# A block's scatters as a list of steps of their own at the end of each slot

## The chip, the cores and the metric

The kernel runs on one core of a Trainium2 chip. The metric is the device time of one execution in microseconds, where lower is better. A core has a matrix engine (TensorE, PE in the profile, with its weight loads as PEld), a vector engine (VectorE, DVE), a scalar engine (ScalarE, ACT) and a general engine (GpSimd, POOL). Each works through its own queue of instructions in order. SyncE (SP) issues most of the transfers; POOL issues the indirect ones, in which every row has an address of its own.

## The reference

The reference is one Macaron layer on 4096 tokens with 256 features:

```python
x = x + 0.5 * ffn(layernorm(x))
x = x + attention(layernorm(x))
x = x + 0.5 * ffn(layernorm(x))
```

The attention works in groups of 64 tokens with 16 heads of 16 features, a causal mask, and an RMS norm over q and over k with a learned weight. The same FFN is used twice. It is a mixture of experts:

```python
shared = silu(x @ sg) * (x @ su) @ sd                   # hidden width 2048
probs  = softmax(rmsnorm(x) @ router_w.T)               # 8 experts
topk_p, topk_i = top_k(probs, 2)
rw     = topk_p / sum(topk_p)
dispatch[e] = first 640 of the tokens that chose e      # capacity 640
eout   = silu(xg @ rg[e]) * (xg @ ru[e]) @ rd[e]        # xg = x[dispatch], width 1024
routed = scatter_add(eout * rw) ; ffn = shared + routed
```

## The kernel before

Every large product is made of three float16 products. An operand is split into a high part (`hi`, a cast on ACT) and a low part (`lo`, the difference between the value and its high part, on DVE or POOL), and the pairs hi·hi, hi·lo and lo·hi are summed in PSUM.

The 4096 tokens are 8 blocks of 512, and a block is 4 tiles of 128. There are four phases. In phase a the shared expert of the first FFN runs over blocks 0 to 3, while all 32 tiles go through the layer norm, the split, the transposition and the router. Phase b runs the first FFN's eight experts. Phase c runs the shared expert over blocks 4 to 7 of the first FFN and 0 to 6 of the second, while the 32 tiles go through the attention, the second layer norm and the second router. Phase d runs the second FFN's experts and its last shared block.

A shared block (`shared`) is a loop over 16 chunks of 128 hidden features. For each chunk `gate_up` makes two PSUM tiles `pgu` (L336). In phase a ACT takes the SiLU of the first (L347); in phase c it takes a tanh (L343) and DVE combines it (L344). DVE multiplies by the second (L349), ACT casts the high part `hh` (L351), DVE makes the low part `hl` (L352). The down product (`down`, L360) is put off behind the next chunk's gate and up. It adds into two PSUM accumulators `po`, which DVE reads at the end of a block (`xr`, L393).

Beside the shared expert run the tiles. Each tile is a list of steps (`tile1` in phase a, `attn_tile` with `tile2` in phase c), written as a generator. A slot (`Tiles.steps`) advances every list that is under way by one step. A new list begins every second slot in phase a (`GAP_A`) and every fourth in phase c (`GAP_C`). `drive` interleaves the main loop with the steps of a slot, two at a time, so the order in which the program is written mixes the two. The build then lets a scheduler set each engine's order from a model of the engines' times; `tc.issue_after(anchor)` keeps an instruction behind another one.

On POOL a tile of phase c has the layer norm's power (`stats`, L149, one for `mv`/`rstd` of the second FFN's norm, one for `amv`/`arstd` of the attention's), the low part of the normalized tile (`two`, L169, tiles `X`, `xa`, `yp`), the power of the q and k norm (L534, tile `ss`), three splits of q and k (L555 twice, L561 once, tile `QK`), the subtraction of the row maximum (L583, tile `S`) and the low part of the exponentials (L594, tile `e16`, `e` in the profile). DVE uses `rstd` in `nm` (L157) and `ss` in L544.

When a block's fourth tile has its router logits, `route` computes the two experts, their weights and the destination row of each token. Its last four steps are the scatters, one for each tile of the block: four copies on POOL put the token's number, its two weights and its expert into the tag columns of the tile `X` (L315), and two indirect transfers on POOL write the tile's rows to the experts' buffer `xg` in HBM (L317). An `X` tile is one of a ring of 16 in phase a and of 6 in phase c, and can be written anew when its two transfers have landed. A scatter stands behind the anchor, which is the last POOL split that the program has written; in phase a there is no such split.

Of the kernel before, what the change touches and what calls it, by code (L numbers as in the profile page):

```python
# [15 lines left out]
ALU = mybir.AluOpType  # L16
# [11 lines left out]
NB = 8  # L28
# [9 lines left out]
class Net:  # L38
# [102 lines left out]
    def stats(self, x, mv, rstd):  # L141
        nc = self.nc
        st = self.sm.tile([P, 6], F32, name="st")
        nc.vector.bn_stats(out=st, in_=x)  # L144
        nc.vector.bn_aggr(out=mv, in_=st)
        ve = self.sm.tile([P, 1], F32, name="ve")
        nc.vector.tensor_scalar(
            out=ve, in0=mv[:, 1:2], scalar1=LN_EPS, scalar2=1.0 / UP ** 2, op0=ALU.add, op1=ALU.mult)
        nc.gpsimd.tensor_tensor(out=rstd, in0=ve, in1=self.mhalf[:, :1], op=ALU.pow)  # L149

    def normed(self, x, mv, rstd, pool=False):

# [69 lines left out]
            fb["L"] = self.sm.tile([P, 4, E], F32, name="L")  # L222
        nc.scalar.copy(fb["L"][:, t, :], p)

    def route(self, R, b, fb):

        nc = self.nc
        sm = self.sm
        mv, rstd = fb["mv"], fb["rstd"]
        rs = sm.tile([P, 4], F32, name="rs")  # L230
        nc.gpsimd.tensor_tensor(out=rs, in0=rstd, in1=rstd, op=ALU.mult)
        nc.gpsimd.tensor_tensor(out=rs, in0=rs, in1=mv[:, :, 1], op=ALU.mult)
        nc.gpsimd.tensor_scalar_add(rs, rs, RMS_EPS * UP ** 2)
        nc.gpsimd.tensor_tensor(out=rs, in0=rs, in1=self.mhalf[:, :4], op=ALU.pow)
        L = fb["L"]
        mx = sm.tile([P, 4, E], F32, name="mx")
        ix = sm.tile([P, 4, E], U32, name="ix")
        for t in range(4):
            nc.vector.max(out=mx[:, t, :], in_=L[:, t, :])
            nc.vector.max_index(out=ix[:, t, :], in_max=mx[:, t, :], in_values=L[:, t, :])  # L240
        dl = sm.tile([P, 4], F32, name="dl")
        nc.vector.tensor_tensor(out=dl, in0=mx[:, :, 1], in1=mx[:, :, 0], op=ALU.subtract)
        nc.gpsimd.tensor_tensor(out=dl, in0=dl, in1=rs, op=ALU.mult)
        nc.gpsimd.tensor_scalar_mul(dl, dl, 1.0 / WS)
        nc.gpsimd.tensor_tensor(out=dl, in0=self.e1, in1=dl, op=ALU.pow)
        w1 = sm.tile([P, 4], F32, name="w1")
        nc.gpsimd.tensor_scalar_add(w1, dl, 1.0)
        nc.gpsimd.tensor_tensor(out=w1, in0=w1, in1=self.mone, op=ALU.pow)
        nc.gpsimd.tensor_scalar_mul(w1, w1, 0.5 / WS)
        nc.gpsimd.tensor_tensor(out=dl, in0=dl, in1=w1, op=ALU.mult)  # L250
        nc.gpsimd.tensor_tensor(out=w1, in0=w1, in1=dl, op=ALU.subtract)
        ef = sm.tile([P, 4, 2], F32, name="ef")
        nc.vector.tensor_copy(ef, ix[:, :, 0:2])
        yield
        oh = sm.tile([P, 4, 2, E], F32, name="oh")
        nc.vector.tensor_tensor(
            out=oh, in0=ef.unsqueeze(3).to_broadcast([P, 4, 2, E]),
            in1=self.iota8.unsqueeze(1).unsqueeze(1).to_broadcast([P, 4, 2, E]), op=ALU.is_equal)
        M = sm.tile([P, 4, E], BF16, name="M")
        nc.vector.tensor_tensor(out=M, in0=oh[:, :, 0, :], in1=oh[:, :, 1, :], op=ALU.add)  # L260
        yield
        pp = self.m1([P, 4, E], F32, "pp")
        nc.tensor.matmul(pp, lhsT=self.tri, rhs=M, start=True, stop=False)
        for t in range(1, 4):
            nc.tensor.matmul(pp[:, t:4], lhsT=self.ones, rhs=M[:, 0:4 - t], start=False, stop=False)
        nc.tensor.matmul(
            pp, lhsT=self.ones, rhs=R["run"].unsqueeze(1).to_broadcast([P, 4, E]), start=False, stop=True)
        n4 = sm.tile([P, E], F32, name="n4")
        nc.vector.tensor_reduce(out=n4, in_=M.rearrange("p t e -> p e t"), axis=AX.X, op=ALU.add)
        nc.vector.tensor_tensor(out=R["run"], in0=R["run"], in1=n4, op=ALU.add)  # L270
        pk = sm.tile([P, 4, 2, E], F32, name="pk")
        nc.vector.tensor_tensor(
            out=pk, in0=oh, in1=pp.unsqueeze(2).to_broadcast([P, 4, 2, E]), op=ALU.mult)
        pos = sm.tile([P, 4, 2], F32, name="pos")
        nc.vector.tensor_reduce(out=pos, in_=pk, axis=AX.X, op=ALU.add)
        yield
        df = sm.tile([P, 4, 2], F32, name="df")
        nc.vector.scalar_tensor_tensor(
            out=df, in0=ef, scalar=float(CAP), in1=pos, op0=ALU.mult, op1=ALU.add)
        nc.vector.tensor_scalar(  # L280
            out=pos, in0=pos, scalar1=float(CAP), scalar2=8192.0, op0=ALU.is_ge, op1=ALU.mult)
        nc.vector.tensor_tensor(out=df, in0=df, in1=pos, op=ALU.add)
        di = sm.tile([P, 4, 2], I32, name="di")
        nc.vector.tensor_copy(di, df)
        yield
        if b == NB - 1:
            self.limits(R)
            yield
        for t in range(4):
            with self.tc.issue_after(self.anchor.ins) if self.anchor else nullcontext():  # L290
                self.scatter(R, b, fb, t, di, w1, dl, ef)
            yield

# [212 lines left out]
    def attn_tile(self, R, j, x2, new_fb):  # L506

        nc = self.nc
# [6 lines left out]
        rstd = self.sm.tile([P, 1], F32, name="arstd")  # L515
# [12 lines left out]
        ss = self.sm.tile([P, 2], F32, name="ss")  # L528
        qk = a.tile([P, 2, H], F32, name="qk", tag="q32")
        for i in range(2):  # L530
            nc.scalar.activation(qk[:, i, :], pqk[:, i, :], AF.Square, scale=1.0 / XP, accum_out=ss[:, i:i + 1])
        nc.vector.tensor_scalar(
            out=ss, in0=ss, scalar1=XP ** 2 / H, scalar2=1e-6 * XP ** 2, op0=ALU.mult, op1=ALU.add)
        nc.gpsimd.tensor_tensor(out=ss, in0=ss, in1=self.mhalf[:, :2], op=ALU.pow)  # L534
        pv = self.m1([P, H], F32, "pv")
        self.project(pv, part, self.wqkv[:, :, :, 2 * H:], TERMS)
        vs = a.tile([P, 2, H], F16, name="vs")
# [2 lines left out]
            out=vs[:, 1, :], in0=pv, scalar=1.0 / XP, in1=vs[:, 0, :], op0=ALU.mult, op1=ALU.subtract)  # L540
        yield
        yield
        for i in range(2):
            nc.vector.scalar_tensor_tensor(  # L544
                out=qk[:, i, :], in0=pqk[:, i, :], scalar=ss[:, i:i + 1], in1=self.lnw,
                op0=ALU.mult, op1=ALU.mult)
        QS = self.QK[:, 0:16].rearrange("p (j s) (r a c) -> p j s r a c", s=2, r=2, a=4)
        for i in range(2):
            if i == 0:
                for r in range(2):  # L550
# [5 lines left out]
                        out=s[:, :, 2:4, :], in0=src, in1=s[:, :, 0:2, :], op=ALU.subtract)  # L556
            else:
# [4 lines left out]
                    out=s[:, :, 1::2, :], in0=src, in1=s[:, :, 0::2, :], op=ALU.subtract)  # L562
        yield
        QT = a.tile([P, 2, 24, 64], F16, name="QT")
        for g in range(2):
            nc.sync.dma_start_transpose(
                out=QT[:, g], in_=self.QK[g * 64:(g + 1) * 64].rearrange("p j c -> p (j c)"))
# [3 lines left out]
        for g in range(2):  # L571
            p = self.m1([P, 8, 64], F32, "psc")
            for jj in range(8):
# [4 lines left out]
                out=S[:, g * 8:(g + 1) * 8, :], in0=p,  # L578
                in1=self.mask.unsqueeze(1).to_broadcast([P, 8, 64]), op=ALU.add)
# [4 lines left out]
            out=S, in0=S, in1=mx.unsqueeze(2).to_broadcast([P, 16, 64]), op=ALU.subtract)  # L584
# [16 lines left out]
        for g in range(2):  # L601
# [7 lines left out]
            for r in range(2):  # L609
                sl = slice(r * 64, (r + 1) * 64)  # L610
                nc.vector.tensor_tensor(
                    out=Y[sl, g], in0=py[sl, :, r * 16:(r + 1) * 16],
                    in1=rc[sl].unsqueeze(2).to_broadcast([64, 8, 16]), op=ALU.mult)
# [58 lines left out]
class Tiles:  # L672
# [7 lines left out]
        self.nxt = 0  # L680

    def done(self):
        return self.nxt == self.count and not self.live

    def steps(self):

        if self.slot == self.nxt * self.gap and self.nxt < self.count:
            self.live.append(self.make(self.nxt))
            self.nxt += 1
        for g in list(self.extra):  # L690
            r = next(g, "end")
            if r == "end":
                self.extra.remove(g)
            elif r != "stall":
                yield
        for g in list(self.live):
            r = next(g, "end")
            if r == "end":
                self.live.remove(g)
            elif r == "stall":  # L700
                return
            yield
        self.slot += 1

# [35 lines left out]
def macaron(ctx, tc, x, w_qkv, ln_w, w_proj, router_w, rg, ru, rd, sg, su, sd, out):  # L740
    nc = tc.nc
    x = x.rearrange("b s h -> (b s) h")
    out = out.rearrange("b s h -> (b s) h")
    n = Net(ctx, tc)
# [4 lines left out]
    fbs = {}  # L749
# [11 lines left out]

    def tail(R, h, b, t):
        if t == 3:
            yield from n.route(R, b, fbs[(h, b)])

    def tile1(j):
        b, t = divmod(j, 4)
        y = n.load_tile(x, b, t)
        yield
        yield  # L770
        if b >= NA:
            nc.sync.dma_start(out=R1["acc"][j * P:(j + 1) * P], in_=y)
        yield from n.front_steps(y, t, new_fb(1, b))
        yield from tail(R1, 1, b, t)
        if j == 31:
            yield from n.expert_load(R1, 0, first[0])

    def tile2(j):
        b, t = divmod(j, 4)
        yield from n.attn_tile(R1, j, x2 if b < NC else out, new_fb(2, b))  # L780
        yield from tail(R2, 2, b, t)
        if j == 31:
            yield from n.expert_load(R2, 0, first[1])
# [8 lines left out]
    with n.phase("a", BT, 2, 16):  # L792
# [5 lines left out]
        tiles = Tiles(tile1, 32, GAP_A)  # L798
# [9 lines left out]
    with n.phase("c", BT, 2, 6, SLC):  # L808
        n.attn_init(w_qkv, ln_w, w_proj)
        tiles = Tiles(tile2, 32, GAP_C)  # L810
# [51 lines left out]
```

## Time and profile before

| | before |
|---|---|
| median of 3 runs | 1830.85 us (1830.73 to 1833.56) |
| the profiled execution | 1834.82 us |
| its span in the trace | 1833.1 us |
| mean granted clock of PE | 0.998 |
| PE busy | 1779.5 us |
| DVE busy | 1199.9 us |
| ACT busy | 952.9 us |
| POOL busy | 751.3 us |

The profile is of one execution. Its span leaves out 1.7 us of that execution's time, and busy times are sums over the span. The scatters' transfers take this much of POOL:

```profile
L317 POOL DMA_INDIRECT xg<-X,di x128 | 132.3, 1034 | 70.4 <-issue 27.5
```

In such a row stand the line, the engine and the operation, what is written from what, the number of instructions, then busy us, the mean ns of one, and last the engine's idle time just before them with what ended most of it. There are 128 of them: two transfers for each of 32 tiles in each of the two FFNs.

### The profile page before, as it was taken

The page shows a single profiled execution, that of the slowest core. Times are in us where ns is not written, and L with a number is a line of the kernel's source. Part 1 is how long each engine was busy: PE and PEld are TensorE (multiplying, and loading weights), DVE is VectorE, ACT ScalarE, POOL GpSimd, SP SyncE. Part 2 cuts the span into 40 slices and gives each one's busy share as a digit, 9 for nine tenths or more (in the row PEclk, how much of TensorE's full clock was granted, in tenths as well). Part 3 has the DMA queues.
Part 4 walks back from the last instruction along what each step waited for, and adds up shares of the span by engine and source line. Part 5 has one row for each costly group of instructions (what it writes and reads, how often), then busy time and mean ns, then how long its engine had stood idle before and what let it go on. Part 6 is the DMA issues. An engine that isn't in the chain of part 4 may idle for free.

```text
span 1833.1 us, 37526 instructions
## 1 busy us (share of the span) xinstructions
PE 1779.5 (97%) x13724; PEld 1197.0 (65%) x13724; DVE 1199.9 (65%) x2891; ACT 952.9 (52%) x2055; POOL 751.3 (41%) x1072
## 2 busy tenths in 40 slices
PE   7899999999999899999999999999999999999998
PEld 4555556777777556666666666665655677777765
DVE  7754445666666567878777878787656566666643
ACT  5433234555555366666666666666323455555542
POOL 6755530112211334567767676776430011112210
PEclk9999999999999999999999999999999999999999
DMA  7532042455543346668576776766213044455420
GB/s 219 146 90 77 3 88 54 107 118 124 118 113 90 73 77 112 122 118 146 113 146 124 133 142 117 144 101 126 52 27 80 28 111 111 107 120 122 102 47 12
DMA packets 439194, 185.96 MB, mean 101 GB/s; under 512 B 302305, under 2 KB 436125, under 8 KB 439008
## 3 DMA queue, kind: packets, MB, share of 16 engines
q1 hardware_dynamic: 420528, 161.60, 40.7%
q0 software_dynamic: 17664, 21.17, 6.5%
q8 instruction: 107, 1.75, 0.4%
q10 hardware_dynamic: 816, 0.79, 0.1%
q14 instruction: 79, 0.65, 0.1%
HBM read 78.95 MB, written 42.21 MB: 66 GB/s over the span
## 4 chain that ended last, share of the span: by engine, by line
PE 36%; issue 32%; POOL 12%; DVE 10%; DMA 5%; ACT 4%; SPq 0%; POOLq 0%; another core or an unknown queue 0%; DVEq 0%; ACTq 0%
PE pgu L336 22%; PE po L360 11%; POOL xg L317 3%; DVE sl L349 2%; DMA acc<-eo,eidscatter 2%; DVE sl L344 1%; DVE hl L352 1%; POOL X L315 1%; POOL rstd L149 1%; POOL acc L459 1%; ACT hh L351 1%; PE pqk L636 1%; POOL S L583 1%; DVE st L144 1%; POOL e L594 1%
## 5 line engine op out<-in xcount | busy, mean ns | idle before, releaser
L336 PE MATMUL pgu<-xb,sgu 128*128 128x512 f16 x3072 | 742.4, 380 | 18.1 <-DVE sl L349 7.7
L351 ACT CAST hh<-sl 128x512 f16<-128x512 f32 (+2 forms) x512 | 272.8, 533 | 482.9 <-DVE sl L349 466.6
L336 PE MATMUL pgu<-xe,wc 128*128 128x384 f16 (+1 forms) x3072 | 497.0, 299 | 0.0
L336 PEld LDWEIGHTS <-sgu 128*128 128x128 f16 x3072 | 293.4, 98 | 292.9 <-issue 25.8
L349 DVE SCALAR_TENSOR_TENSOR sl<-pgu,sl 128x512 f32<-128x512 f32 (+2 forms) x512 | 300.2, 587 | 227.3 <-PE pgu L336 193.4
L352 DVE TENSOR_TENSOR hl<-sl,hh 128x512 f16<-128x512 f32 (+2 forms) x512 | 311.2, 608 | 161.5 <-ACT hh L351 155.1
L360 PEld LDWEIGHTS <-hh 128*128 128x128 f16 x3328 | 320.3, 98 | 112.3 <-ACT hh L351 7.9
L336 PEld LDWEIGHTS <-wc 128*128 128x128 f16 x3072 | 300.5, 98 | 92.0
L360 PE MATMUL po<-sdw,hh 128*128 128x256 f16 x2048 | 350.1, 273 | 8.1 <-issue 2.8
L360 PE MATMUL po<-sdw,hl 128*128 128x256 f16 x1024 | 247.1, 273 | 14.3 <-DVE hl L352 13.4
L360 PE MATMUL po<-wd,hh 128*128 128x256 f16 x1280 | 223.6, 273 | 0.0
L459 POOL DMA_INDIRECT out_dram<-eo,eidscatter x40 | 65.1, 1627 | 342.1 <-DVE eo L458 332.3
L360 PEld LDWEIGHTS <-hl 128*128 128x128 f16 x1664 | 162.8, 98 | 58.6 <-DVE hl L352 24.2
L347 ACT ACTIVATE sl<-pgu 128x384 f32<-128x384 f32 (+1 forms) x336 | 158.9, 473 | 71.1 <-PE pgu L336 35.5
L459 POOL DMA_INDIRECT acc<-eo,eidscatter x40 | 65.7, 1643 | 296.5 <-DVE eo L458 286.8
L317 POOL DMA_INDIRECT xg<-X,di x128 | 132.3, 1034 | 70.4 <-issue 27.5
L360 PE MATMUL po<-wd,hl 128*128 128x256 f16 x640 | 152.5, 273 | 1.1 <-DVE hl L352 1.1
L344 DVE SCALAR_TENSOR_TENSOR sl<-sl,pgu 128x512 f32<-128x512 f32 x176 | 119.9, 681 | 48.1 <-ACT sl L343 46.1
L343 ACT ACTIVATE sl<-pgu 128x512 f32<-128x512 f32 x176 | 104.2, 593 | 45.3 <-PE pgu L336 39.7
L104 ACT ACTIVATE wc<-re 128x512 f16<-128x512 f32 x128 | 80.5, 629 | 67.9 <-PE pgu L336 57.6
L105 DVE SCALAR_TENSOR_TENSOR wc<-re,wc 128x512 f16<-128x512 f32 x128 | 88.3, 690 | 22.9 <-ACT wc L104 22.6
L583 POOL TENSOR_TENSOR S<-S,amx 128x1024 f32<-128x1024 f32 x32 | 62.0, 1938 | 79.0 <-DVE amx L582 72.1
(150 smaller groups left out, 1713.3 us busy)
## 6 DMA issues: line engine op xcount, KB each, us to landing
re<-in_L_ffn_rg_dram SPq DMA_DIRECT2D x128, 128.0 KB
re<-in_L_ffn_ru_dram SPq DMA_DIRECT2D x128, 128.0 KB
re<-in_L_ffn_rd_dram SPq DMA_DIRECT2D x128, 128.0 KB
y<-acc SPq DMA_DIRECT2D x64, 128.0 KB
y<-in_L_attn_x_dram SPq DMA_DIRECT2D x32, 128.0 KB
acc<-xr SPq DMA_DIRECT2D x16, 256.0 KB
out_dram<-xr SPq DMA_DIRECT2D x16, 256.0 KB
x<-y SPq DMA_DIRECT2D x28, 128.0 KB
```

The lines of the kernel that those rows point to most:

```text
L104: nc.scalar.mul(hi, src, WS)
L105: nc.vector.scalar_tensor_tensor(out=lo, in0=src, scalar=WS, in1=hi, op0=ALU.mult, op1=ALU.subtract)
L317: i = nc.gpsimd.indirect_dma_start(out=R["xg"][:, :], out_offset=bass.IndirectOffsetOnAxis(ap=di[:, t, k:k + 1], axis=0), in_=X, in_offset ...
L336: nc.tensor.matmul(p, lhsT=wc[:, w, i, k, :], rhs=x[:, 2 * a + k, :], start=(j == 0), stop=(j == 5))
L343: nc.scalar.activation(s, p, AF.Tanh, scale=0.5 / XP)
L344: nc.vector.scalar_tensor_tensor(out=s, in0=s, scalar=1.0, in1=p, op0=ALU.add, op1=ALU.mult)
L347: self.latest[0] = nc.scalar.activation(s, p, AF.Silu, scale=1.0 / XP).ins
L349: self.latest[1] = nc.vector.scalar_tensor_tensor(out=s, in0=ps[1], scalar=1.0 / XP / (2.0 * XP if tanh else 1.0), in1=s, op0=ALU.mult, op ...
L351: nc.scalar.copy(h[0], s)
L352: nc.vector.tensor_tensor(out=h[1], in0=s, in1=h[0], op=ALU.subtract)
L360: nc.tensor.matmul(o, lhsT=h[a][:, t * P:(t + 1) * P], rhs=wd[:, w], start=(c == 0 and j == 0 and t % 2 == 0), stop=(c == nch - 1 and j == 2),
L459: i = nc.gpsimd.indirect_dma_start(out=R["acc"][:, :], out_offset=bass.IndirectOffsetOnAxis(ap=ids[:, t:t + 1], axis=0), in_=eo, in_offset ...
```

## The change

The four scatters of a block become a list of steps of their own (`scatters`). For the blocks 0 to 6 `route` hands this list to the tiles' `extra` lists; for block 7 it still runs them as its own last steps. In a slot the lists under way are now advanced first, and each extra list is advanced by one step at the end of the slot, so one scatter is written per slot. Before, extra lists (none were used) came first. The tiles are done only when the extra lists are, too. The anchor is now also set by the powers of L149 and of L534, so a scatter stands behind the last power or split of its slot on POOL, and every scatter has an anchor, in phase a too.

```diff
@@ stats
-        nc.gpsimd.tensor_tensor(out=rstd, in0=ve, in1=self.mhalf[:, :1], op=ALU.pow)
+        self.anchor = nc.gpsimd.tensor_tensor(out=rstd, in0=ve, in1=self.mhalf[:, :1], op=ALU.pow)
@@ route
-    def route(self, R, b, fb):
+    def route(self, R, b, fb, tiles):
...
+        last = self.scatters(R, b, fb, di, w1, dl, ef)
+        if b == NB - 1:
+            yield from last
+        else:
+            tiles.extra.append(last)
+
+    def scatters(self, R, b, fb, di, w1, dl, ef):
+
         for t in range(4):
-            with self.tc.issue_after(self.anchor.ins) if self.anchor else nullcontext():
+            with self.tc.issue_after(self.anchor.ins):
                 self.scatter(R, b, fb, t, di, w1, dl, ef)
             yield
@@ attn_tile
-        nc.gpsimd.tensor_tensor(out=ss, in0=ss, in1=self.mhalf[:, :2], op=ALU.pow)
+        self.anchor = nc.gpsimd.tensor_tensor(out=ss, in0=ss, in1=self.mhalf[:, :2], op=ALU.pow)
@@ Tiles
     def done(self):
-        return self.nxt == self.count and not self.live
+        return self.nxt == self.count and not self.live and not self.extra
...
-        for g in list(self.extra):
-            r = next(g, "end")
-            if r == "end":
-                self.extra.remove(g)
-            elif r != "stall":
-                yield
         for g in list(self.live):
             r = next(g, "end")
             if r == "end":
                 self.live.remove(g)
             elif r == "stall":
                 return
             yield
+        for g in list(self.extra):
+            if next(g, "end") == "end":
+                self.extra.remove(g)
+            yield
         self.slot += 1
```

More of the change, by code (lines that the diff above doesn't have):

```diff
@@ L763, in tail @@
         if t == 3:
-            yield from n.route(R, b, fbs[(h, b)])
+            yield from n.route(R, b, fbs[(h, b)], tiles)
     def tile1(j):
```

## Prediction

> **What bounds the kernel now.** I read the busy shares first, then what TensorE (PE) waits for, then the same microseconds on the engines behind those waits. Columns of the page's first part: busy us, share of the span, instructions.
>
> ```profile
> span 1833.1 us, 37526 instructions
> PE 1779.5 (97%) x13724; PEld 1197.0 (65%) x13724; DVE 1199.9 (65%) x2891; ACT 952.9 (52%) x2055; POOL 751.3 (41%) x1072
> ```
>
> PE is the bound. GpSimd (POOL), which the change rearranges, is busy 41%. The change can shorten only PE's idle time, 1833.1 − 1779.5 = 53.6 us, and only where a POOL result ends the wait. Windows by stage (columns: window, length, then busy us of PE, weight loads, DVE, ACT, POOL, each with its instructions; then the PE clock, the DMA share, GB/s):
>
> ```profile
> 0.00:130.00 130.00, 109.14 (x722) 63.57 (x723) 92.34 (x327) 56.04 (x126) 89.39 (x212) 0.99 0.56 159
> 290.00:605.00 315.00, 314.72 (x2506) 244.90 (x2505) 191.75 (x403) 167.36 (x394) 57.81 (x35) 1.00 0.45 105
> 815.00:1290.00 475.00, 464.87 (x3969) 294.67 (x3967) 374.53 (x941) 310.05 (x649) 335.70 (x470) 1.00 0.69 129
> 1420.00:1833.00 413.00, 407.47 (x3078) 300.47 (x3075) 231.91 (x464) 197.51 (x444) 65.08 (x40) 1.00 0.37 84
> ```
>
> PE idles 20.9 us before 130 and 10.1 us in 815:1290, where POOL is busiest (71%). The expert stages (second row; fourth, which ends with a shared block) hold no moved scatter. PE's waits in 815:1290, then in 75:130 (us in total, times, longest):
>
> ```profile
> PE pgu L336 <- DVE sl L344: 5.2, 6, 0.9
> PE po L360 <- DVE hl L352: 4.9, 8, 0.7
> ```
> ```profile
> PE pgu L336 <- DVE sl L349: 2.4, 1, 2.4
> ```
>
> Six blocks of about 81 us each lose one gap to L344 and one to L352. The timeline of one of them, PE, then POOL, then DVE (start, us, engine, line, operation; in brackets the idle time before and who ended it):
>
> ```profile
> 846.25 1.46 PE L336 MATMUL pgu<-xb,sgu 128*128 128x512 f16 x6 [0.87 <-DVE sl L344]
> 849.44 0.28 PE L360 MATMUL po<-sdw,hl 128*128 128x256 f16 x1 [0.71 <-DVE hl L352]
> ```
> ```profile
> 835.09 0.99 POOL L317 DMA_INDIRECT xg<-X,di  x1 [0.17 <-POOL S L583]
> 836.38 0.97 POOL L317 DMA_INDIRECT xg<-X,di  x1 [0.30 <-issue]
> ...
> 838.01 2.15 POOL L594 TENSOR_TENSOR e<-S,e 128x1024 f16<-128x1024 f32 x1
> 840.10 0.57 POOL L149 TENSOR_TENSOR rstd<-ve,mhalf 128x1 f32<-128x1 f32 x1
> 840.65 0.54 POOL L149 TENSOR_TENSOR arstd<-ve,mhalf 128x1 f32<-128x1 f32 x1
> 843.02 0.70 POOL L534 TENSOR_TENSOR ss<-ss,mhalf 128x2 f32<-128x2 f32 x1 [1.83 <-DVE ss L532]
> ```
> ```profile
> 845.51 0.69 DVE L344 SCALAR_TENSOR_TENSOR sl<-sl,pgu 128x512 f32<-128x512 f32 x1 [0.55 <-ACT sl L343]
> ...
> 848.10 0.68 DVE L393 SCALAR_TENSOR_TENSOR xr<-po,xr 128x512 f32<-128x512 f32 x1
> 848.70 0.68 DVE L352 TENSOR_TENSOR hl<-sl,hh 128x512 f16<-128x512 f32 x1
> ```
>
> Read back from gap 1: L344 waits for ACT's L343, which stands behind the QK casts; those wait for L544, that for the ss power (843.02 to 843.72). The power waits for L532, that for ACT's squares (841.92), queued behind two z's that wait for the layer norm's powers at 840.10. Those stand behind e, and e behind the scatter pair. So a scatter pair is on the path of gap 1. Gap 2 is another thing: hl sits behind two xr (L393) and an S on DVE.
>
> **The change part by part.** No instruction is added or removed, so the sum of busy times stays and only order counts. Each scatter moves as four tag copies (0.66 + 3 × 0.17, overlapping to 0.5 to 1.1 us) and two indirect DMAs of 0.97 to 1.1 us with 0.3 us between: a pair holds POOL about 2.45 us. Comparing the two builds' orders:
>
> (1) Up to 290 us. The scatters keep their places among the powers; 32 tag copies of 0.17 us each move behind powers, at a cost of nothing: POOL idles here (66.8 of 160 us busy in 130:290), and if that cover went it would be 32 × 0.17 = 5 us of POOL time. What shifts is DVE's order at 112 us, where PE loses 2.39 us: before, L349 stands behind an X split that waits 3.08 us for a scatter's DMA to release its tile (112.46). After, that L349 is ahead of it, but the next cast hh still stands behind an X cast on ACT (112.02), so about 1.4 us of gap stays: −1.0. Two other L349/L352 move later by about 0.6 us into stretches that wait for scatters anyway: 0. What the gap does to the clock is the second place for a price:
>
> ```profile
> 113.50:117.20 3.70, 3.59 (x16) 2.04 (x16) 2.31 (x7) 2.09 (x5) 0.18 (x1) 0.58 0.36 71
> ```
>
> Row: in the 3.7 us after a gap of 2.39 us PE had 0.58 of its clock, 0.42 × 3.7 = 1.6 us lost. [...] The row shows a drop at less idle, so a 1.4-us gap may still drop it: I take 0.5. Part sum −1.5; ends −3 and +1.5 (the 0.6-us shifts landing on PE twice).
>
> (2) Stages that keep their order: 290 to 815 and from 1320 on (the last block's scatters and the expert loads are unchanged): 0.
>
> (3) Six blocks of 815:1320, 24 scatters. Before, one block runs on POOL: e, scatter 0, two powers, ss, X, QK, scatter 1, xa, QK, scatter 2, S, scatter 3, yp, e, two powers, ss, X, xa. After: e, two powers, scatter 0, X, ss, xa, scatter 1, QK, QK, S, scatter 2, yp, e, two powers, scatter 3, X, ss, xa. I step the new order with the old durations in the block of 897 to 927 (81.1 us after the lines above; times in that block). e ends 897.4; powers to 898.5; copies and scatter 0 to 901.7; X, ss, xa to 903.8; scatter 1 to 906.9; QK and QK to 909.4; copies to 909.9; S waits for its maximum (910.05) and ends 912.0, where before it ended 916.0; scatter 2 to 914.6; yp, e to 917.4; copies to 917.9. The powers now wait for their variance (837.43 + 0.15 + 81.1 = 918.7) and end 919.85, where before they ended 922.3. So 2.4 us are won there, and almost given back: scatter 3 holds POOL until 922.4, X until 923.1, and ss ends at 923.8 instead of 843.72 + 81.1 = 924.8. One us reaches L344: done at about 926.3 instead of 927.3, and PE is free at 845.38 + 81.1 = 926.5. Gap 1 goes from 0.87 to 0 to 0.3: −0.75.
>
> Gap 2: DVE's new order is L349, hl, xr, S, xr. hl no longer waits for xr, −0.71; but the next block's down matmuls take the two accumulators that the xr's release, now one operation later each, with hl waiting 0.6 us for its cast. The first costs about 0.4 us, the second about 0.65: +1.05. Balance +0.2 (PE's shortfall after 848 is 0.87 in all, counted by matmul cadence). Net per block −0.55, times six −3.3. Ends: both gaps gone, −1.8 a block (−11); gap 1 kept and gap 2 grown, +0.7 a block and a little more on other waits (+7).
>
> Newly placed waits: DVE's nm (L157), which waits for POOL's rstd, is now ahead of an L349, with hh (ACT), hl and PE behind that; ACT's exp of S stands ahead of an L343, 1.2 to 1.9 us later. PE has about 1 us in hand at both: 0 taken, up to +0.7 a block if it is not there, inside the end above.
>
> [...]
>
> ```profile
> L352 DVE TENSOR_TENSOR hl<-sl,hh x95: 656/691/1392, 816.6 to 1288.4; 128x512 f16<-128x512 f32 x95
> ```
>
> Row: the median is 0.69 us, and the few that meet a split take 1.0 to 1.4, so a new meeting costs 0.3 to 0.7. [...] The splits' own moves make as many meetings disappear as appear; I take 0 and keep +2 in the range.
>
> SP issues the same transfers with some swaps of y loads and x2 stores; it was not last in any wait of PE: 0, by the cover of the slots between load and use.
>
> Sum: −1.5 − 3.3 = −4.8. Profiled execution 1834.82 (span 1833.1 and 1.72 around it), so 1830.0 there. That execution lies 3.97 above the median 1830.85 of the runs, so I predict 1830.85 − 4.8 = 1826.0.
>
> **The rivals.**
> A, the forecast: 1826 (1823 to 1829).
> B, no change: gap 1 closes and the accumulators' wait takes its whole place; 1830.85 − 1 to + 2. For it: PE's order is nearly the same, and 97% is busy. Against: the second wait is worked out at 0.2 net.
> C, more: both gaps go and the cold clock stays away: −11 − 3, 1817. For it: S and the powers come 4 and 2.4 us earlier. Against: two xr need 1.3 us of DVE before two accumulators are free.
> D, slower: scatter 3 stands between the powers and ss, X. If its start waits, or the pair takes over 1.0 us more than 2.45, ss ends after 924.8 and gap 1 is larger than before, while gap 2 keeps its +0.2 and nm holds L349. At +1.25 a block, +7.5: 1838. It decides at the 1.0 us. For it: the old order had ss free of any scatter, and pairs in the trace take from 2.3 to 2.8 us. Against: 2.4 us were won just ahead.
> That the change does not do what it says holds up to 290 us, where scatters hardly move; it leaves −3.3, inside A and B.
>
> **How the numbers follow.** A measurement tells about 0.2% (3.7 us) from no change. A 0.40, of which 0.32 beyond 3.7 us; C 0.08; B 0.20; D 0.32, since an order that only a model of the engines chose has more ways to be late than early. Faster 0.40, same 0.28, slower 0.32. The range 1817 to 1840 leaves out C's far half and D's tail; A's own is 1823 to 1829.
>
> **What would show it.** Right: in 815:1290 the waits on L344 fall below 2 us, L360 waits name xr L393, S runs about 4 us earlier in its block, powers 2.4, ss 1.0; the gap at 113 us is 1.4. Wrong: ss later than in the old place, PE waiting on L349 behind nm, or POOL pairs above 3 us; or a PE idle sum in the six blocks above 10.1 us.

## The result and the profile after

The changed kernel takes 1838.43 us (median of 9 runs, 1835.70 to 1840.28) against 1832.81 us (9 runs) for the kernel before: a ratio of 1.0026, 95% interval 1.0017 to 1.0036. It is slower by about 5 us, where the forecast was a gain of 4.8 us. The profiled execution is the lowest of the nine, 1835.70 us, with a span of 1834.0; the one of before was 1834.82, above its median. So the two traces differ in length by less than the medians do, and stages have to be compared one by one.

The page of the changed kernel, busy us and share of the span:

```profile
span 1834.0 us, 37526 instructions
PE 1780.6 (97%) x13724; PEld 1198.3 (65%) x13724; DVE 1220.1 (67%) x2891; ACT 949.9 (52%) x2055; POOL 762.7 (42%) x1072
```

The same instructions keep DVE busy 20 us longer and POOL 11 us longer. Nothing was added, so some of them last longer than before. The windows say where (same columns as in the windows of before):

```profile
0.00:130.00 130.00, 110.78 (x737) 64.62 (x738) 94.57 (x331) 56.72 (x127) 89.72 (x213) 0.99 0.57 159
815.00:1290.00 475.00, 460.42 (x3927) 291.60 (x3926) 390.26 (x925) 302.75 (x640) 340.48 (x462) 1.00 0.69 127
1420.00:1833.00 413.00, 409.15 (x3092) 302.06 (x3090) 233.09 (x465) 199.11 (x446) 65.51 (x40) 1.00 0.37 84
```

In 815:1290 DVE has 15.7 us more busy time (374.53 before) and PE 4.5 us less in the same time. PE's waits in that window:

```profile
PE po L368 <- DVE xr L401: 5.4, 12, 0.5
PE pgu L344 <- DVE sl L352: 3.5, 6, 0.6
PE po L368 <- DVE hl L360: 3.0, 6, 0.9
PE psc L582 <- DVE vs L547: 2.7, 7, 0.5
```

From L290 on lines are 8 higher than before: L352 here is the tanh combination that was L344, L360 is hl, L401 is xr, L547 is vs, L542 is ss, L602 is e. Gap 1 (L352) is a third smaller, gap 2 is now the wait for the two xr, and the waits of six hl and seven vs stand beside them. The gap on L352 comes back every 81.91 us, (1249.55 − 840.01) / 5, where before it was (1250.09 − 846.25) / 5 = 80.77 (the last gap of before first, then those of the changed kernel):

```profile
1250.09 1.46 PE L336 MATMUL pgu<-xb,sgu 128*128 128x512 f16 x6 [0.87 <-DVE sl L344]
```
```profile
840.01 1.46 PE L344 MATMUL pgu<-xb,sgu 128*128 128x512 f16 x6 [0.59 <-DVE sl L352]
922.18 1.45 PE L344 MATMUL pgu<-xb,sgu 128*128 128x512 f16 x6 [0.59 <-DVE sl L352]
...
1249.55 0.81 PE L344 MATMUL pgu<-xb,sgu 128*128 128x512 f16 x3 [0.59 <-DVE sl L352]
```

In this pair of traces that is 1.14 us a block and 6.8 us in six, against −3.3 in the forecast.

What lasts longer is hl. Its row in the source view (min/median/max ns), 691 and 1392 in the kernel before:

```profile
L360 DVE TENSOR_TENSOR hl<-sl,hh x93: 651/693/2206, 820.0 to 1287.8; 128x512 f16<-128x512 f32 x93
```

The busy time of hl in 815:1290 is 87.50 us, where it was 70.52. The timeline of one of the long ones, POOL first, then DVE, then PE:

```profile
932.23 2.13 POOL L602 TENSOR_TENSOR e<-S,e 128x1024 f16<-128x1024 f32 x1 [1.30 <-ACT e L601]
936.52 0.54 POOL L149 TENSOR_TENSOR rstd<-ve,mhalf 128x1 f32<-128x1 f32 x1 [2.16 <-DVE ve L147]
...
939.97 0.70 POOL L542 TENSOR_TENSOR ss<-ss,mhalf 128x2 f32<-128x2 f32 x1
```
```profile
932.71 2.20 DVE L360 TENSOR_TENSOR hl<-sl,hh 128x512 f16<-128x512 f32 x1 [0.32 <-ACT hh L359]
934.83 0.74 DVE L144 BATCH_NORM_STATS2 st<-y 128x6 f32<-128x256 f32 x2
...
940.71 0.48 DVE L552 SCALAR_TENSOR_TENSOR qk<-pqk,ss,lnw 128x256 f32<-128x256 f32 x1 [1.03 <-POOL ss L542]
941.11 0.42 DVE L547 SCALAR_TENSOR_TENSOR vs<-pv,vs 128x256 f16<-128x256 f32 x1
```
```profile
941.58 0.39 PE L582 MATMUL psc<-QT 128*128 128x64 f16 x8 [0.47 <-DVE vs L547]
```

The hl starts 0.48 us after POOL's e and ends at 934.91, 0.55 us after e's end at 934.36. hl reads both its operands from SBUF, as e does; by these times hl stood still until POOL's e was over, and then took most of its usual 0.69 us. (In this program what PE writes stands in PSUM; all other tiles on the chip stand in SBUF.) All 17 hl of the six blocks that start beside an e end 0.55 to 0.65 us after that e, though they start from 0.47 to 1.48 us into it. Behind this hl stand the statistics of the next tile, behind them the powers on POOL, then ss, then qk, which DVE's new queue has ahead of vs; PE then waits 0.47 us for vs at 941.58.

POOL was held beside an hl as well. The ss power of the block's last scatter slot took 1.21 us instead of 0.70, beside an hl that had begun 0.45 us earlier; in the six blocks it took 1.20 to 1.22 us:

```profile
917.98 1.07 DVE L360 TENSOR_TENSOR hl<-sl,hh 128x512 f16<-128x512 f32 x1
918.43 1.21 POOL L542 TENSOR_TENSOR ss<-ss,mhalf 128x2 f32<-128x2 f32 x1
```

That is why gap 1 did not close. In all six blocks of both traces the matmul of gap 1 starts 2.53 to 2.54 us after the end of ss (here 918.43 + 1.21 = 919.64, and 922.18), so the 0.5 us by which hl held up ss are 0.5 us of this gap.

### The profile page after: what moved, and what is told of

It reads as the page before. It is cut to its first block, busy times and chain, and to the rows that moved or that the text cites. A ratio compares the mean times of both kernels' runs of the same rounds, so it can differ in the third digit from the quotient of the medians.

```text
span 1834.0 us, 37526 instructions
## 1 busy us (share of the span) xinstructions
PE 1780.6 (97%) x13724; PEld 1198.3 (65%) x13724; DVE 1220.1 (67%) x2891; ACT 949.9 (52%) x2055; POOL 762.7 (42%) x1072
## 4 chain that ended last, share of the span: by engine, by line
PE 44%; issue 19%; POOL 13%; DVE 12%; DMA 6%; ACT 4%; SPq 1%; POOLq 0%; another core or an unknown queue 0%; DVEq 0%; ACTq 0%
PE pgu L344 28%; PE po L368 14%; POOL xg L325 3%; DVE hl L360 2%; DVE sl L357 2%; DVE sl L352 2%; POOL X L323 1%; DMA acc<-eo,eidscatter 1%; ACT hh L359 1%; DMA QT<-QK 1%; POOL ss L542 1%; DVE S L585 1%; DVE amx L590 1%; POOL QK L563 1%; POOL acc L467 1%
## 5 line engine op out<-in xcount | busy, mean ns | idle before, releaser
L344 PE MATMUL pgu<-xb,sgu 128*128 128x512 f16 x3072 | 741.7, 380 | 13.1 <-DVE sl L352 5.6
L344 PE MATMUL pgu<-xe,wc 128*128 128x384 f16 (+1 forms) x3072 | 497.0, 299 | 0.0
L344 PEld LDWEIGHTS <-sgu 128*128 128x128 f16 x3072 | 293.8, 98 | 287.8 <-issue 20.9
L357 DVE SCALAR_TENSOR_TENSOR sl<-pgu,sl 128x512 f32<-128x512 f32 (+2 forms) x512 | 300.6, 587 | 222.6 <-PE pgu L344 192.1
L360 DVE TENSOR_TENSOR hl<-sl,hh 128x512 f16<-128x512 f32 (+2 forms) x512 | 329.6, 644 | 161.9 <-ACT hh L359 154.0
L344 PEld LDWEIGHTS <-wc 128*128 128x128 f16 x3072 | 300.6, 98 | 92.0
L368 PE MATMUL po<-sdw,hl 128*128 128x256 f16 x1024 | 249.6, 273 | 10.3 <-DVE hl L360 10.0
L352 DVE SCALAR_TENSOR_TENSOR sl<-sl,pgu 128x512 f32<-128x512 f32 x176 | 119.8, 681 | 35.1 <-ACT sl L351 33.5
```

Source lines behind the costliest of these rows:

```text
L344: nc.tensor.matmul(p, lhsT=wc[:, w, i, k, :], rhs=x[:, 2 * a + k, :], start=(j == 0), stop=(j == 5))
L352: nc.vector.scalar_tensor_tensor(out=s, in0=s, scalar=1.0, in1=p, op0=ALU.add, op1=ALU.mult)
L357: self.latest[1] = nc.vector.scalar_tensor_tensor(out=s, in0=ps[1], scalar=1.0 / XP / (2.0 * XP if tanh else 1.0), in1=s, op0=ALU.mult, op ...
L360: nc.vector.tensor_tensor(out=h[1], in0=s, in1=h[0], op=ALU.subtract)
L368: nc.tensor.matmul(o, lhsT=h[a][:, t * P:(t + 1) * P], rhs=wd[:, w], start=(c == 0 and j == 0 and t % 2 == 0), stop=(c == nch - 1 and j == 2),
```

## The experiments

Three theories were set against each other; the third is rival D of the prediction. Lock: DVE operations with two SBUF inputs, hl above all, and POOL's splits hold each other up, and the new order brings more of them together. Order: the new queue of DVE (qk ahead of vs, the row maximum ahead of hl, xr behind hl) makes PE wait, whatever the durations. Late ss: scatter 3 ahead of ss keeps gap 1, and nothing else is lost. Every run below was timed beside the kernel before on the same chip, and a difference is that of the two medians. The kernel before had medians of 1831.38, 1831.49 and 1834.38 us in the three sets of runs, so differences from different sets can be off against each other by a few us.

**The phases alone.** One flag keeps the new list and anchors out of phase a, or out of phase c.

```diff
-        if b == NB - 1:
+        if b == NB - 1 or not tiles.late:       # late: gap == GAP_C for c_only, GAP_A for a_only
             yield from last
...                                              # and the powers set the anchor in that phase only
```

c_only: 

> The change in phase c alone (the end-of-slot lists and the powers as anchors there; phase a as before). The traces put +7.5 us of PE's idle time into phase c and -5 us into phase a, where executions differ. If phase c is the whole cause: +5 to +8 us against the kernel before. If the scatters of phase a are the cause: within 2 us of it.

Measured: 1836.41 against 1831.38 us, ratio 1.0029 (1.0017 to 1.0041), +5.0 us.

a_only: 

> The change in phase a alone, phase c as before. If phase c is the whole cause: -2 to +1 us against the kernel before. If phase a takes part: +3 us or more, or -4 us or less where the shorter phase a of the changed kernel's trace was the change's doing.

Measured: 1830.43 against 1831.38 us, ratio 0.9993 (0.9987 to 1.0000), −1.0 us. The loss comes from phase c. For phase a the interval is −2.4 to 0 us: it takes in what part (1) of the prediction had (−1.5), and just touches nothing at all.

**The halves of the change in phase c.** In list_only the two powers there do not set the anchor; in anchor_only they do, and the scatters of phase c are still the last steps of `route`.

```diff
-        self.anchor = nc.gpsimd.tensor_tensor(out=ss, in0=ss, in1=self.mhalf[:, :2], op=ALU.pow)
+        nc.gpsimd.tensor_tensor(out=ss, in0=ss, in1=self.mhalf[:, :2], op=ALU.pow)   # list_only, and L149 in phase c
...
-        if b == NB - 1:
+        if b == NB - 1 or not tiles.late:       # anchor_only, late: gap == GAP_A
```

list_only: 

> The end-of-slot lists in both phases, but in phase c only the splits set the anchor. POOL's order moves much as in the changed kernel (the two layer norm powers ahead of a scatter pair, scatter 3 between the powers and ss), while DVE's queue keeps the order of before in phase c: hl ahead of the maximum, vs ahead of qk, both xr ahead of hl. Theory lock (hl, held up beside POOL's split of e, makes the loss): the e splits start as early as in the changed kernel, hl's busy time in phase c rises by 10 us or more, +4 to +8 us. Theory order (DVE's new queue makes the loss: qk behind POOL's ss ahead of vs, the maximum ahead of hl, xr behind hl): -3 to +1 us. Theory late ss (scatter 3 ahead of ss keeps gap 1 and nothing else is lost): 0 to +3 us, with the waits on L344 as large as before.

Measured: 1834.09 against 1831.38 us, ratio 1.0014 (1.0007 to 1.0020), +2.7 us. This lies below the +4 to +8 of the lock and above the order's +1, and by the time alone it would fit the late ss. The waits decide. PE's in 815:1290, and hl's row (line numbers are three higher than in the changed kernel):

```profile
PE po L371 <- DVE hl L363: 10.3, 13, 1.0
PE po L371 <- DVE ve L148: 1.9, 6, 0.3
PE pgu L347 <- DVE sl L355: 1.4, 6, 0.2
```
```profile
L363 DVE TENSOR_TENSOR hl<-sl,hh x94: 656/692/2712, 816.3 to 1288.9; 128x512 f16<-128x512 f32 x94
```

With hl, vs and xr in their old places of DVE's queue, gap 1 nearly goes (5.2 to 1.4 us in the window), as the forecast had it, although scatter 3 stands ahead of ss here too: the late ss falls. But the waits for hl double, 4.9 to 10.3, and hl's busy time in the window is 102.17 us, 31.7 more than before. This loss comes without DVE's new order, so that order can't be its reason.

anchor_only: 

> The powers set the anchor in phase c, but a block's scatters stay the last steps of route, as before (phase a as in the changed kernel). POOL's order stays close to that of before: scatter 0 ahead of the powers, scatter 3 ahead of yp and e. All three theories: -2 to +2 us against the kernel before, hl's busy time as before. If the anchor itself costs time: +3 us or more.

Measured: 1844.15 against 1831.38 us, ratio 1.0069 (1.0055 to 1.0083), +12.8 us, which no theory had foreseen in its numbers. The timeline, POOL, DVE, PE and ACT, and then ACT in the kernel before:

```profile
918.62 0.70 POOL L169 TENSOR_TENSOR yp<-Y,yp 128x256 f16<-128x256 f32 x1
919.25 2.14 POOL L602 TENSOR_TENSOR e<-S,e 128x1024 f16<-128x1024 f32 x1
```
```profile
918.90 3.06 DVE L360 TENSOR_TENSOR hl<-sl,hh 128x512 f16<-128x512 f32 x1 [2.43 <-ACT hh L359]
```
```profile
922.01 0.28 PE L368 MATMUL po<-sdw,hl 128*128 128x256 f16 x1 [2.26 <-DVE hl L360]
```
```profile
917.30 1.04 ACT L601 CAST e<-S 128x1024 f16<-128x1024 f32 x1
918.25 0.61 ACT L359 CAST hh<-sl 128x512 f16<-128x512 f32 x1
```
```profile
917.00 0.60 ACT L351 CAST hh<-sl 128x512 f16<-128x512 f32 x1
917.50 1.04 ACT L593 CAST e<-S 128x1024 f16<-128x1024 f32 x1
```

ACT has its cast of e ahead of its cast hh here, where the kernel before has hh first. So hl starts at 918.90 instead of 917.63 (in the trace of before, which is at nearly the same place there), inside POOL's yp. It is not let in between yp and e, and ends at 921.96, 0.57 us after e. PE waits 2.26 us for it, once a block. The exchange of two casts stands at the head of this wait; it was not tried alone.

**The lock taken away, the order held.** In phase c L349 writes its product back into its PSUM tile, so that hl reads one operand from PSUM and one from SBUF. Edges that only fix the issue order hold each kernel's five queues in the order recorded of the same kernel without the edit; in the traces DVE, ACT and POOL have exactly the old order.

```diff
-            out=s, in0=ps[1], scalar=..., in1=s, op0=ALU.mult, op1=ALU.mult).ins
+            out=ps[1] if tanh else s, in0=ps[1], scalar=..., in1=s, op0=ALU.mult, op1=ALU.mult).ins
+        s = ps[1] if tanh else s
         nc.scalar.copy(h[0], s)
         nc.vector.tensor_tensor(out=h[1], in0=s, in1=h[0], op=ALU.subtract)
...
+        hold(tc)      # add_manual_dep(b, a.name, NoSync) for each pair of neighbours in a recorded queue
```

before_psum_hl: 

> The kernel before, every engine's queue held in its recorded order, with one edit in phase c: L349 writes the activated hidden chunk back into its PSUM tile instead of the SBUF tile sl, so hl reads one operand from SBUF instead of two. Theory lock (a DVE operation with two SBUF inputs waits for POOL's splits and the other way round): hl's few long cases (1.0 to 1.4 us) go, its busy time in six blocks falls by 4 to 5 us, and since PE waits for hl behind xr here, -2 to +1 us. Theory order (the queues' order alone matters): 0, within 1.5 us. Control for the next three.

Measured: 1827.19 against 1831.49 us, ratio 0.9977 (0.9966 to 0.9988), −4.3 us: more gain than either theory had. hl's busy time fell as expected, but the edit also frees the tile `sl` earlier; how much of the 4.3 us that is was not tried.

after_psum_hl: 

> The changed kernel, queues held in its own recorded order on all five engines, with the same edit of L349 and hl. Theory lock: hl is 0.7 us everywhere, DVE's busy time in phase c falls by 17 us or more, PE's gaps behind hl, vs and L344 shrink, and the time falls by 4 to 8 us against the changed kernel: -2 to +2 us against the kernel before. Theory order: hl gets shorter and PE's gaps stay, because qk still waits for ss ahead of vs and the maximum still stands ahead of hl: +4 to +7 us against the kernel before.

Measured: 1825.20 against 1831.49 us, ratio 0.9967 (0.9955 to 0.9980), −6.3 us. hl's row, and the only wait of PE that the view still lists in 815:1290:

```profile
L362 DVE TENSOR_TENSOR hl<-pgu,hh x96: 650/690/693, 816.4 to 1288.7; 128x512 f16<-128x512 f32 x96
```
```profile
PE pgu L344 <- DVE hl L362: 5.5, 12, 0.8
```

The longest hl is 693 ns. As many hl start beside an e as in the changed kernel, 17, and none of them is held. With the long hl went the waits for vs, xr and L352 in the very same queues; what is left is PE waiting for the PSUM tile that hl now reads. Theory order had +4 to +7 us here; the lock's −2 to +2 was missed too, on the fast side, as in the control. From +5.6 us to −6.3 us the edit is worth 11.9 us in the changed kernel and 4.3 us in the kernel before. The 7.6 us between them, with an uncertainty of some 3.5 us by the three intervals, are what the lock costs the changed kernel more than the kernel before; they cover the whole loss of 5.6 us.

list_psum_hl: 

> The kernel with end-of-slot lists but without the powers as anchors in phase c, queues held in its own order, with the same edit. It had lost gap 1 (waits on L344 1.4 us) and got longer waits for hl (10.3 us in six blocks). Theory lock: those waits fall to 3 to 5 us and the time to -3 to -7 us against the kernel before, faster than both kernels: the gain that was forecast for gap 1, without the lock. Theory order: as without the edit, +2 to +3 us.

Measured: 1828.28 against 1831.49 us, ratio 0.9986 (0.9979 to 0.9992), −3.2 us: 5.9 us less than without the edit. PE's waits for hl do not fall as forecast: they are 6.2 us, now for its PSUM tile.

anchor_psum_hl: 

> The kernel with the powers as anchors in phase c and the scatters as last steps of route (+12.8 us), queues held in its own order, with the same edit. Its trace has hl of 3.06 us once a block, started inside POOL's yp and ending 0.57 us after POOL's e. Theory lock: that hl takes 0.7 us, the 2.3-us gap goes, and the time is within 2 us of the kernel before. Theory order: +10 us or more stays.

Measured: 1825.61 against 1831.49 us, ratio 0.9965 (0.9952 to 0.9979), −5.9 us: 18.7 us less than without the edit, in the same queues, and 1.6 us below the control. With one SBUF input, four orders that lay 12.8 us apart lie within 3.1 us.

**e's share, and the scheduler's own order.**

```diff
-        self.anchor = nc.gpsimd.tensor_tensor(out=e16[:, :, 1, :], in0=S, in1=e16[:, :, 0, :], op=ALU.subtract)
+        self.anchor = nc.gpsimd.memset(e16[:, :, 1, :], 0.0)      # after_zero_e
```

after_zero_e: 

> The changed kernel, all queues held in its own recorded order, with POOL's split of e (L594) replaced by a memset of the low half to zero: the low part of the exponentials is left out, and the operation reads no SBUF. Theory lock, as a clash of two readers of SBUF: the 17 hl beside e take 0.7 us instead of 1.2 to 2.2, hl's busy time in six blocks falls by about 15 us, and the time falls by 4 to 7 us against the changed kernel (the later splits also come earlier by the 2 us that e no longer takes). If hl waits for any busy POOL, hl beside the memset stays long in proportion to the memset. If the lock is not what costs: within 2 us of the changed kernel.

Measured: 1824.59 against 1834.38 us, ratio 0.9947 (0.9933 to 0.9960), −9.8 us. Against the changed kernel's +5.6 this is 15 us less, over twice the 4 to 7 us that were expected. The memset takes POOL less than half of e's time and waits for no cast, so POOL's chain is shorter as well, and the gain is not the lock's alone:

```profile
L602 POOL MEMSET e<- 128x1024 f16 x24 | 22.9, 954 | 0.0
```
```profile
L360 DVE TENSOR_TENSOR hl<-sl,hh x97: 656/693/1225, 816.9 to 1288.6; 128x512 f16<-128x512 f32 x97
```

The cases up to 2.2 us are gone; those of 1.2 us stand beside S, which still reads SBUF (the hl at 907.05 took 1.23 us and ended 0.56 us after the S of 905.83). Whether hl would wait for a POOL operation that only writes was not shown.

after_psum_free: 

> The changed kernel with L349 writing into PSUM in phase c, queues as the scheduler sets them. hl has one SBUF input, so no order can hit the lock with it: hl 0.7 us everywhere; if the gain comes from the lock and not from the held order, -3 to -7 us against the kernel before, as with the order held.

Measured: 1824.55 against 1834.38 us, ratio 0.9952 (0.9938 to 0.9966), −9.8 us, more than expected; the longest hl is again 693 ns.

before_psum_free: 

> The kernel before with L349 writing into PSUM in phase c, queues as the scheduler sets them: -2 to -6 us against the kernel before, as with the order held. Beside the run before it, it tells what the change is worth where the lock can't strike: forecast -5 to 0.

Measured: 1830.46 against 1834.38 us, ratio 0.9980 (0.9972 to 0.9988), −3.9 us. Where hl can't be held up, the change is worth 1824.55 − 1830.46 = −5.9 us (forecast −5 to 0), and the two intervals do not meet; with the queues held it was 1825.20 − 1827.19 = −2.0 us, where the intervals overlap. The prediction's −4.8 us lies between the two, but neither confirms it: in the free pair the scheduler has set other queues than in the two kernels that the prediction compares, and the held pair can't be told from no change. The changed kernel with hl's operand in PSUM is the version that beats both kernels.

## Why the prediction was wrong

Right: PE is the bound and phase c decides. Part (1), −1.5 us for phase a, against −1.0 measured; the gap at 113 us shrank from 2.39 to 0.97 us (1.4 had been worked out), and PE's clock was 1.00 behind it instead of 0.58. The 0.5 us taken for the clock was the author's estimate, and no run shows it: in the changed kernel's trace two gaps of 1.11 and 1.25 us close together (up to 83.83 and 85.67 us) brought a clock of 0.55 at 86.5 to 90 us, where before it was 1.00, and in c_only, whose phase a is that of before, the clock of 0:290 was 1.00 against 0.99 in the kernel before. Part (2): the expert stages did not move. The steps on POOL: moved by the 4.87 us between PE's gaps in the two traces (926.46 and 921.59), e was to end at 912.5, the powers at 915.0 and ss at 918.9; they ended at 913.3, 915.3 and 919.6. ss was thus not later than in its old place (924.8 − 4.87 = 919.9), and no pair took over 2.8 us; of the signs of being wrong the one that came was PE's idle sum, 475 − 460.42 = 14.6 us instead of 10.1.

Gap 1, −0.75 a block: the mechanism was right, as list_only shows (5.2 to 1.4 us in the window, −0.6 a block). In the changed kernel the gap shrank by only 0.28 us (0.87 to 0.59), because hl beside the ss power held it for 0.5 us.

Gap 2, +0.2 a block: about right. The two xr keep PE waiting 0.52 and 0.38 us, where before hl behind them kept it 0.71.

The step that failed is the price of POOL's splits beside hl: "I take 0 and keep +2 in the range". The +2 is one new meeting a block at 0.3 us, in six blocks; no run shows it. The step had two errors. First the price of a meeting, 0.3 to 0.7 us, was read off a row of minimum, median and maximum. The 1.07-us cases of the kernel before all started 1.61 us into an e of 2.13 us: 0.52 us of waiting and 0.55 us of work. So these hl too waited for e's end, and had only come late in it; an hl that came 0.48 us into an e took 2.20 us. In the changed kernel 17 of 17 waited to e's end. Second the count: meetings were said to appear and to vanish in equal number. In six blocks the long meetings with e rose from 6 to 17, and hl's busy time from 70.5 to 87.5 us, 14 of the 17 us beside e. With the 0 fell the premise that "the sum of busy times stays": the same instructions kept DVE busy 20 us and POOL 11 us longer.

The waits newly placed on DVE and ACT were taken as 0. They came to nothing in the runs with hl's operand in PSUM. In the changed kernel they passed hl's delay on: a late hl makes the statistics late, then the powers, ss, qk and vs behind it. PE's gaps for vs (two in a block, 0.18 and 0.47 us) and for hl (0.42 us) come behind such a chain, and went with the long hl in after_psum_hl.

Rival D had the sign and, with 1838, the very time, but by luck: its condition did not come true. The scatter pair ahead of ss took 2.33 us, ss was not later, and list_only shows that scatter 3 ahead of ss costs nothing by itself.

## What to carry to other kernels

Before moving work between queues, list the pairs of VectorE and GpSimd operations that could come to lie beside each other and of which a trace shows one held by the other, and price a meeting at the whole rest of the other operation. Here the VectorE operation was hl, with two SBUF inputs, and a meeting with e made it last up to 2.21 us instead of 0.69. To see whether a long duration is such a block, compare its end with the end of what ran on the other engine: a fixed distance (here 0.55 to 0.65 us) is the sign, and an average hides it. If one of the two operands can stay in PSUM, as hl's did here, the block can go (no hl over 693 ns in this kernel), at the price of a PSUM tile held longer (PE waited 5.5 us for it in six blocks).

## What the runs showed of the hardware

hl also waited for other POOL operations than e. In the changed kernel's trace the hl at 907.06 started 1.19 us into an S of 1.89 us, took 1.25 us and ended 0.55 us after it; the one at 917.98 started 0.17 us into a split of L169 (tile `X`) that took 0.68 us, took 1.07 us and ended 0.56 us after it. In anchor_only the hl at 918.90 waited through the end of yp and the whole of e that followed it, 3.06 us. Not every POOL operation held it: in the kernel before, the hl at 860.92 started 0.43 us into a power of 128x4 elements that took 1.05 us (L234), and took 0.69 us. Of DVE's operations of the same 128x512 elements, L352 and L357 of the changed kernel read one operand from PSUM; in 815:1290 they took at most 0.69 us.

PE's clock fell after gaps of 2.39 us (the kernel before, at 113 us) and 2.26 us (anchor_only), and not after all of them. In anchor_only the same gap of 2.26 us comes six times, and four times the clock falls. The fall that the rows below show lasts 3.41 us at a clock of 0.50. The four begin at 922.97, 1004.89, 1172.14 and 1254.06 us, which are 81.92, 167.25 and 81.92 us apart: 24, 49 and 24 times 3.413. In the kernel before, the clock is 0.50 from 114.08 to 117.49 us and from 1830.98 on, 1716.90 us or 503 times 3.4133 later; in the changed kernel from 86.24 to 89.65 us and from 1833.87 on, 1747.63 us or 512 times 3.4133 later. So in each of these three traces the falls begin a whole number of such lengths apart. The first gap of anchor_only (836.43 to 838.70) and the second (919.75 to 922.01), in stretches of 3.41 us counted back from the first fall (the clock is the third number from the end, PE's busy time the second number of a row):

```profile
834.21:837.62 3.41, 1.96 (x12) 0.80 (x9) 2.04 (x1) 1.83 (x3) 3.27 (x3) 1.00 0.81 209
837.62:841.03 3.41, 2.33 (x24) 1.82 (x25) 2.76 (x9) 0.68 (x2) 1.55 (x3) 1.00 0.51 95
919.56:922.97 3.41, 1.15 (x11) 0.87 (x10) 3.31 (x6) 0.00 (x0) 2.64 (x3) 1.00 0.31 72
922.97:926.38 3.41, 3.41 (x19) 1.81 (x18) 1.84 (x6) 2.72 (x9) 0.39 (x2) 0.50 1.01 190
```

The first gap falls on two stretches, PE is busy 1.96 and 2.33 us in them, and the clock stays. The second lies in one stretch, PE is busy 1.15 of its 3.41 us, and the clock is 0.50 in the next. The traces of the two kernels fit: before the fall at 114.08 us of the kernel before PE was busy 1.02 us (110.67:114.08), before the fall at 86.24 us of the changed kernel 1.17 us (82.83:86.24), and in the changed kernel the clock stayed at 1.00 behind a stretch with 1.49 us (1383.30:1386.71). At which busy time the fall begins was not tried. By estimate a fall costs 0.5 × 3.41 = 1.7 us, four of them 6.8 us; with the 7.2 us by which PE was busy less in 815:1290 (457.71 against 464.87) that makes 14.0 us, about the 12.8 us that anchor_only lost (its profiled execution lay 1.6 us above its median).
